# One idle step between the rounding and the transposes of the attention's output layer, for the first two batch elements

## The chip, the cores and the metric

The kernel runs on one core of one Trainium2 chip. The metric is the device time of one execution, in microseconds (us). The profile is one execution recorded by the hardware profiler. Engines: PE is TensorE (matmuls and transposes; PEld its weight loads), DVE is VectorE, ACT is ScalarE, POOL is GpSimd, SP issues DMAs. L231 is line 231 of the kernel before.

## The reference, cut to what matters

Four batch elements of 512 tokens by 512 channels pass through two layers, each with a mixing part and a feed-forward part, all residual:

```python
x = x + tanh(g_xattn[0]) * wkv(w, u, layernorm(x), ctx)                 # a recurrence over the tokens
x = x + tanh(g_ffn[0])   * bitlinear_ffn(layernorm(x), w1, w2, w3)      # 1-bit weights, int8 activations in groups of 64
x = x + tanh(g_xattn[1]) * cross_attention(layernorm(x), ctx)           # 16 heads of 32
x = x + tanh(g_ffn[1])   * ternary_linear(rmsnorm(layernorm(x)), W)     # ternary weights, int8 rows
```

The change concerns the end of the cross attention. Its output layer rounds each row of `o` to int8 levels before the product:

```python
def _qdq(x):
    s = jnp.maximum(jnp.max(jnp.abs(x), axis=-1, keepdims=True) / 127.0, 1e-08)
    return jnp.clip(jnp.round(x / s), -127.0, 127.0) * s
...
out = _qdq(o) @ _qdq(wp).T + bp
```

## The kernel before

Tokens lie on the 128 partitions, so one element is four row tiles t0 to t3 of 128 x 512. The four elements run as a pipeline: while the attention of element b is worked on, the feed-forward layer of element b+1 and the WKV recurrence of element b+2 run beside it. Every layer is a Python generator, and each `yield` ends a step. `line(generator, parts)` (L1190 to L1230) gives a generator a list of parts `(start, end, steps)`: step k of a part has the place `start + (end - start) * k / steps`. `run` always advances the line with the least place. One unit of place is one element, divided into `SLOTS` = 17 slots. The places set the order in which steps are written; `in_turn` and `next_turn` (L147 to L159) pin TensorE's instructions to that order, while the framework's scheduler may still order the other engines' instructions among themselves, by their dependences.

**The feed-forward layer** of the next element runs 16 units of one slot each: 8 up matmuls (`ff_hp`) for either branch, gating on ACT and DVE (`ff_z`, L745 to L750), transposes (`tp_ps`) with splitting into two fp32r parts (`hr`, ACT L696 and DVE L697), and 8 down matmuls (`ff_acc`). Its quantiser is `qg_s`, `qg_i`, `qg_b` (L671 to L685), the last step (`ff_z`/`ff_xn` back to float) on POOL. `xp` is the same kind of pair for the next row tile's input.

**The attention** works head by head: `s_ps` scores on TensorE, maximum `at_nm` on DVE (L948), exponential `at_P` on ACT (L950), transposes `pt_ps` with a copy `at_PT` on ACT (L970), values `o_ps` on TensorE with a copy on ACT (L990), a transpose back (`ot_ps`), division by the sums into `at_o` on DVE (L998, L1000). These 72 steps go over 18 slots. After them comes `project_out(t)` (L1017 to L1040), the output layer of one row tile, in three steps:

1. absolute maximum of the row (DVE L222), scale and reciprocal (DVE L226, L227), rounding in place (ACT L231, `at_o`);
2. four transposes into one PSUM bank (`qr_ps`) and their eviction to bf16 (ACT L238, `at_oqT`);
3. four bf16 matmuls (`p_ps`), scaling into `at_y` (DVE L1036), addition to the residual `xb` (POOL L1037 for elements 0 and 1).

`in_steps(chains, 1)` (L240 to L253) staggers the four row tiles by one step, the later tile first within a step. Three steps each, staggered by one, make 6 steps, which the part `(end, end + 2.4 / SLOTS, 6)` spreads over 2.4 slots. So in one step of the whole, t2 is rounded, t1 transposed, and t0 multiplied. Element 2 has an ending of its own with other places (`together`, `end`), element 3 runs with nothing beside it and has the same part of 6 steps.

**The ternary layer** of elements 0 and 1 (L1128 to L1180) follows: statistics of `xb` (DVE L191 to L206), power and normalisation on POOL (L180 to L219, L1147: `tf_xn`), absolute maximum (DVE L222, `tf_s`), rounding, transposes, product. Its line starts 11 slots (element 0) or 3 slots (element 1) after `end`.

**Buffers.** PSUM has eight banks: three with the tag "m", used in rotation by `qr_ps`, `p_ps`, `pt_ps`, `ot_ps`, `tp_ps`, `wy_ps`, `q_ps` and `o_ps`; three with "hp" (`s_ps` and `ff_hp`); two with "acc". An instruction that takes a bank waits for the instruction that last read it. `at_oqT` has two buffers; `at_y` shares the rotating row buffers `at_row` (`ROWS` of them) with `at_xn`, `at_q`, `at_half` and `tf_xn`; the small scale tiles `at_s` have four.

Of the kernel before, what the change touches and what calls it, by code (L numbers as in the profile page):

```python
# [30 lines left out]
def kernel(  # L31
# [37 lines left out]
    NB, T, D = x.shape  # L69
# [61 lines left out]
    def bank(name, dtype=F32):  # L131

        return psum_tile(name, "m", dtype)
# [27 lines left out]
    def matmul(*args, **kwargs):  # L161
        return in_turn(nc.tensor.matmul(*args, **kwargs))  # L162
# [58 lines left out]
    def absmax(dst, src):  # L221
        nc.vector.tensor_reduce(dst, src, AX.X, ALU.max, apply_absolute_value=True)  # L222

    def int8_scale(s, r, amax):

        nc.vector.tensor_scalar(s, amax, 1.0 / 127.0, 1e-8, ALU.mult, ALU.max)  # L226
        nc.vector.reciprocal(r, s)  # L227

    def rounded(src, r):

        nc.scalar.activation(src, src, AF.Identity, bias=magic[:, 0:1], scale=r)  # L231

    def transposed_rows(dst, src):

        pt = bank("qr_ps")
        for c in range(NC):
            transpose(pt[:, c * P : (c + 1) * P], src[:, c * P : (c + 1) * P], ident)
        nc.scalar.activation(dst, blocks(pt), AF.Identity, bias=magic[:, 1:2])  # L238
# [601 lines left out]
    def attention_layer(b, xb, pool, tiles=range(NT)):  # L840
# [15 lines left out]
        def row(name, dtype=F32):  # L856
            return pool.tile([P, D], dtype, name=name, tag="at_row", bufs=ROWS)
# [159 lines left out]
        def project_out(t):  # L1017
            s = sm.tile([P, 2], F32, name="at_s", tag="at_s")
            o = o_all[:, t, :]
            absmax(s[:, 0:1], o)  # L1020
            int8_scale(s[:, 0:1], s[:, 1:2], s[:, 0:1])
            rounded(o, s[:, 1:2])
            yield True
            oqT = pool.tile([P, NC, P], BF16, name="at_oqT", tag="at_oqT")
            transposed_rows(oqT, o)
            yield True
            pp = bank("p_ps")
            for c in range(NC):
                matmul(
                    pp, lhsT=oqT[:, c, :], rhs=wpT[:, c, :], start=(c == 0), stop=(c == NC - 1)  # L1030
                )
            if b > NB - 3:
                y = wk.tile([P, D], F32, name="at_y", tag="wk_v")
            else:
                y = row("at_y")
            nc.vector.scalar_tensor_tensor(y, pp, s[:, 0:1], swp_b, ALU.mult, ALU.mult)  # L1036
            (nc.vector if b > NB - 3 else nc.gpsimd).tensor_tensor(  # L1037
                xb[:, t, :], xb[:, t, :], y, ALU.add
            )
            yield True  # L1040
# [9 lines left out]
        def end(ts):  # L1050

            yield from together([project_out(t) for t in ts])
            means, scale = statistics(b, xb, ts)
            yield from together([ternary(b, xb, pool, t, means, scale) for t in ts])
# [51 lines left out]
        if alone:  # L1106
            yield from ending
        else:
            yield from in_steps([project_out(t) for t in tiles], 1)
# [66 lines left out]
    def ternary_layer(b, xb, pool):  # L1176
        if b == NB - 2:
            r, scale = statistics(b, xb, range(NT))
            yield
        else:  # L1180
            r, scale = layernorm(xb, rms=True, pinned=False), None
        yield from in_steps([ternary(b, xb, pool, t, r, scale) for t in range(NT)], 1)
# [9 lines left out]
    def late(make):  # L1192
        yield from make()
# [26 lines left out]
    SLOTS = NT * NF + 1  # L1220

    def line(gen, *parts, aside=False):
        lines.append({"gen": gen, "parts": parts, "step": 0, "aside": aside})
# [124 lines left out]
    for b in range(NB):  # L1348
        if b:
            early = (0.99, 1.0, 4) if b == 1 else (b - 0.19, b - 0.1, 3), (b - 0.08, b, 1)  # L1350
            line(
                late(lambda b=b: ffn_layer(xs[b])),
                *((early[0],) if b == 1 else early),
                (b, b + 16 / SLOTS, 64),
                (b + 16 / SLOTS, b + 17.75 / SLOTS, 7),
            )
        start = b + 1 + 4.95 / SLOTS
        end = start + 18 / SLOTS
        line(
            late(lambda b=b: attention_layer(b, xs[b], at)),  # L1360
            (b + 1.0 if b == 0 else b + 0.7, b + 1.03 if b == 0 else b + 0.9, 5),
            (b + 1 + 1.7 / SLOTS, b + 1 + 3.7 / SLOTS, 5),
            (b + 1 + 3.75 / SLOTS, b + 1 + 4.35 / SLOTS, 2),
            (start, end, 72),
            (end, end + 2.4 / SLOTS, 6)
            if b != NB - 2
            else (end - 0.15 / SLOTS, end + 4.65 / SLOTS, 6),
            (end + 2.4 / SLOTS, end + 3.4 / SLOTS, 4),
        )
        if b < NB - 1:  # L1370
            late_by = 8 / SLOTS if b == 0 else 0.0
            line(
                late(lambda b=b: ternary_layer(b, xs[b], at)),
                (end + 3 / SLOTS + late_by, end + 8 / SLOTS + late_by, 8)
                if b < NB - 2
                else (end + 4.85 / SLOTS, end + 11.85 / SLOTS, 7),
                aside=b < NB - 2,
            )
# [46 lines left out]
```

## Time and profile before

| what | value |
|---|---|
| median of 3 runs | 1088.22 us (1086.59, 1090.55, 1088.22) |
| the profiled execution, its own time | 1090.16 us |
| its span in the profile | 1088.2 us |
| its mean granted TensorE clock | 0.959 |
| PE busy | 942.7 us (87%) |
| PEld busy | 678.8 us (62%) |
| DVE busy | 828.3 us (76%) |
| ACT busy | 730.4 us (67%) |
| POOL busy | 322.1 us (30%) |
| chain that ended last | PE 46%, DVE 24%, ACT 14%, POOL 6%, DMA 5%, issue 5% |

The profiled execution is 1.94 us above the median and has 1.96 us around its span. "Busy" counts the time in which an engine works on an instruction; matmuls are pipelined, so their ends are modelled. In a timeline a row gives start, duration of the whole group, engine, line, operation, output <- input, the shapes and a count, and in brackets the idle time of the engine just before and the instruction that ended it. "PEclk" or granted clock is the share of full speed that TensorE's throttle allowed. The end of element 0's attention lies at 584 to 622 us of the span, that of element 1 at 796 to 820 us.

### The profile page before, as it was taken

The page shows a single profiled execution, that of the slowest core. Times are in us where ns is not written, and L with a number is a line of the kernel's source. Part 1 is how long each engine was busy: PE and PEld are TensorE (multiplying, and loading weights), DVE is VectorE, ACT ScalarE, POOL GpSimd, SP SyncE. Part 2 cuts the span into 40 slices and gives each one's busy share as a digit, 9 for nine tenths or more (in the row PEclk, how much of TensorE's full clock was granted, in tenths as well). Part 3 has the DMA queues.
Part 4 walks back from the last instruction along what each step waited for, and adds up shares of the span by engine and source line. Part 5 has one row for each costly group of instructions (what it writes and reads, how often), then busy time and mean ns, then how long its engine had stood idle before and what let it go on. Part 6 is the DMA issues. An engine that isn't in the chain of part 4 may idle for free.

```text
span 1088.2 us, 17928 instructions
## 1 busy us (share of the span) xinstructions
PE 942.7 (87%) x6351; PEld 678.8 (62%) x6380; DVE 828.3 (76%) x1600; ACT 730.4 (67%) x1490; POOL 322.1 (30%) x328
## 2 busy tenths in 40 slices
PE   3869997998978889889997898999999999878975
PEld 2335565565657666677775576777777777655652
DVE  5985548757876799897769799978687766579977
ACT  6656756566545776768777577777675767877863
POOL 3831104412433154621215536314022410100000
PEclk8889999998999999999999799999999999989998
DMA  8178945364454673745566446564683663244311
GB/s 290 39 254 323 327 167 205 136 221 166 155 138 164 229 252 103 257 117 158 211 204 211 146 150 200 155 235 146 221 242 117 207 215 93 73 132 118 115 41 39
DMA packets 85672, 189.67 MB, mean 174 GB/s; under 512 B 12240, under 2 KB 36816, under 8 KB 74576
## 3 DMA queue, kind: packets, MB, share of 16 engines
q1 hardware_dynamic: 85584, 188.53, 52.7%
q8 instruction: 51, 0.84, 0.3%
q14 instruction: 37, 0.30, 0.1%
HBM read 148.65 MB, written 39.85 MB: 173 GB/s over the span
## 4 chain that ended last, share of the span: by engine, by line
PE 46%; DVE 24%; ACT 14%; POOL 6%; DMA 5%; issue 5%; SPq 0%; ACTq 0%; POOLq 0%; DVEq 0%
PE ff_hp L162 13%; PE pt_ps L165 7%; PE ff_acc L162 5%; PE o_ps L162 4%; PE v_ps L162 4%; PE s_ps L162 3%; ACT at_P L950 3%; DVE wk_q L640 3%; DVE at_nm L948 3%; ACT at_PT L970 2%; PE k_ps L162 2%; DVE ff_z L750 1%; DVE qg_i L680 1%; DVE wk_p L634 1%; PE tp_ps L165 1%
## 5 line engine op out<-in xcount | busy, mean ns | idle before, releaser
L162 PE MATMUL ff_hp<-wT,xp 128*128 128x512 f32 x1024 | 273.9, 410 | 7.7 <-DVE ff_z L746 4.6
L162 PEld LDWEIGHTS ff_hp<-wT,xp 128*128 128x128 f32 x1024 | 194.1, 194 | 54.9 <-DVE ff_z L746 6.1
L950 ACT ACTIVATE at_P<-s_ps,at_nm 128x512 f32<-128x512 f32 x256 | 175.2, 691 | 45.3 <-DVE at_nm L948 43.6
L948 DVE TENSOR_REDUCE at_nm<-s_ps 128x1 f32<-128x512 f32 x256 | 166.5, 678 | 37.6 <-PE s_ps L162 37.3
L970 ACT COPY at_PT<-pt_ps 128x512 f32<-128x512 f32 x224 | 131.4, 591 | 73.3 <-PE pt_ps L165 72.6
L685 POOL TENSOR_TENSOR ff_z<-qg_b,qg_s 128x512 f32<-128x512 bf16 x64 | 72.7, 1135 | 314.6 <-ACT qg_b L684 291.0
L165 PE MATMUL pt_ps<-ident,at_P 128*128 128x128 f32 x1024 | 156.2, 282 | 9.0 <-ACT at_PT L970 4.9
L165 PEld LDWEIGHTS pt_ps<-ident,at_P 128*128 128x128 f32 x1024 | 119.1, 143 | 47.4 <-ACT at_PT L970 12.5
L162 PE MATMUL ff_acc<-wT,hr 128*128 128x512 f32 x512 | 137.1, 408 | 7.3 <-ACT hr L696 3.8
L162 PE MATMUL s_ps<-at_kR,at_qR 128*128 128x512 f32 x256 | 103.8, 467 | 27.4 <-ACT at_P L950 20.2
L162 PEld LDWEIGHTS ff_acc<-wT,hr 128*128 128x128 f32 x512 | 92.0, 189 | 28.7 <-DVE hr L697 5.6
L162 PE MATMUL o_ps<-at_PT,at_V 128*32 128x128 f32 x2048 | 75.6, 281 | 5.0 <-ACT at_PT L970 3.2
L162 PEld LDWEIGHTS o_ps<-at_PT,at_V 128*32 128x32 f32 x2048 | 55.0, 111 | 28.6 <-issue 11.4
L745 ACT ACTIVATE ff_z<-ff_hp,coef 128x512 f32<-128x512 f32 x64 | 44.1, 689 | 41.6 <-PE ff_hp L162 39.3
L746 DVE SCALAR_TENSOR_TENSOR ff_z<-ff_z,ff_hp 128x512 f32<-128x512 f32 x64 | 43.4, 678 | 37.2 <-ACT ff_z L745 36.8
L750 DVE SCALAR_TENSOR_TENSOR ff_z<-ff_hp,coef,ff_z 128x512 f32<-128x512 f32 x64 | 47.7, 746 | 29.2 <-PE ff_hp L162 28.8
L162 PEld LDWEIGHTS s_ps<-at_kR,at_qR 128*128 128x128 f32 x256 | 43.7, 195 | 41.6 <-ACT at_P L950 28.6
L684 ACT CAST qg_b<-qg_i 128x512 bf16<-128x512 int8 x80 | 49.3, 617 | 26.6 <-DVE qg_i L680 19.0
L162 PE MATMUL v_ps<-wkvT,cT 128*128 128x512 f32 x128 | 60.4, 618 | 5.6 <-DVE wT L303 2.3
L162 PE MATMUL k_ps<-cT,wkvT 128*128 128x512 f32 x128 | 60.5, 624 | 2.4 <-ACT wk_k L584 1.0
L640 DVE RECIPROCAL wk_q<-wk_q 128x256 f32<-128x256 f32 x32 | 54.5, 1722 | 2.9 <-POOL wk_q L635 1.5
L950 ACT ACTIVATION_READ_ACCUMULATOR at_P<-s_ps,at_nm 128x1 f32 x256 | 52.0, 203 | 0.0
(180 smaller groups left out, 1656.1 us busy)
## 6 DMA issues: line engine op xcount, KB each, us to landing
wT<-wD SPq DMA_DIRECT2D x72, 1024.0 KB, 5.6
wn<-in_L_ffn_w_dram SPq DMA_DIRECT2D x18, 1024.0 KB, 6.5
at_kR<-kD SPq DMA_DIRECT2D x128, 128.0 KB, 4.9
at_qR<-qD SPq DMA_DIRECT2D x256, 64.0 KB, 2.4
wD<-wT SPq DMA_DIRECT2D x12, 1024.0 KB, 4.5
kD<-k_half SPq DMA_DIRECT2D x16, 512.0 KB, 2.8
qD<-at_half SPq DMA_DIRECT2D x32, 256.0 KB, 2.1
cn<-in_ctx_dram SPq DMA_DIRECT2D x8, 512.0 KB, 6.2
```

What stands on the lines that cost most here:

```text
L162: return in_turn(nc.tensor.matmul(*args, **kwargs))
L165: return in_turn(nc.tensor.transpose(*args))
L634: nc.vector.tensor_tensor_scan(p[:, 1:], A2, E2, 0.0, ALU.mult, ALU.add)
L640: nc.vector.reciprocal(half, half)
L684: nc.scalar.copy(qb, qi)
L685: nc.gpsimd.tensor_tensor(grouped(src), grouped(qb), s.unsqueeze(2).to_broadcast([P, NG, GS]), ALU.mult)
L745: nc.scalar.activation(z, hp, AF.Tanh, scale=coef[:, 0:1])
L746: nc.vector.scalar_tensor_tensor(z, z, 1.0, hp, ALU.add, ALU.mult)
L750: nc.vector.scalar_tensor_tensor(z, hp, coef[:, 1:2], z, ALU.mult, ALU.mult)
L948: nc.vector.tensor_reduce(nm, sp, AX.X, ALU.max, negate=True)
L950: nc.scalar.activation(lanes[k, i, t], sp, AF.Exp, bias=nm, accum_out=sums[k][:, t, i : i + 1],)
L970: made[k] = nc.scalar.copy(dst, blocks(pt))
```

## The change

`project_out` gets one more `yield` after the rounding, for elements 0 and 1 only (`b < NB - 2`, with `NB` = 4). The step between the two yields holds no instruction. With four steps each, staggered by one, the four row tiles now make 7 steps, and the part is lengthened from 2.4 to 2.8 slots, so that a step still takes 0.4 of a slot. In one step of the whole, t3 is rounded, t2 does nothing, t1 is transposed and t0 is multiplied. Elements 2 and 3 keep their parts of 6 steps. The four leftover steps of the last part and the ternary layer's places are as before.

```diff
@@ project_out
             int8_scale(s[:, 0:1], s[:, 1:2], s[:, 0:1])
             rounded(o, s[:, 1:2])
             yield True
+            if b < NB - 2:
+                yield True
             oqT = pool.tile([P, NC, P], BF16, name="at_oqT", tag="at_oqT")
             transposed_rows(oqT, o)
             yield True
@@ the attention's line
             (start, end, 72),
-            (end, end + 2.4 / SLOTS, 6)
-            if b != NB - 2
+            (end, end + 2.8 / SLOTS, 7)
+            if b < NB - 2
+            else (end, end + 2.4 / SLOTS, 6)
+            if b == NB - 1
             else (end - 0.15 / SLOTS, end + 4.65 / SLOTS, 6),
             (end + 2.4 / SLOTS, end + 3.4 / SLOTS, 4),
```

## The prediction

> **What bounds the kernel now.** I read the table of engines first: TensorE is busy for 87% of the span, VectorE for 76%. The chain of waits over the whole span gives PE 46%, DVE 24%, ACT 14%: the bound changes hands. So the two places that the change touches were read by themselves: the end of element 0's attention (584 to 626 us) and of element 1's (796 to 835 us).
>
> TensorE's timeline at the first place (start, duration, tile, count; in brackets the idle time before it and what ended it):
>
> ```profile
> 594.90 0.60 PE L165 MATMUL wy_ps<-ident,wk_e 128*128 128x128 f32 x4
> 599.34 1.11 PE L165 MATMUL qr_ps<-ident,at_o 128*128 128x128 f32 x4 [3.84 <-ACT at_o L231]
> 600.25 1.91 PE L162 MATMUL p_ps<-wpT,at_oqT 128*128 128x512 bf16 x4
> 602.09 1.94 PE L162 MATMUL o_ps<-at_PT,at_V 128*32 128x128 f32 x32
> 603.96 0.95 PE L165 MATMUL pt_ps<-ident,at_P 128*128 128x128 f32 x4
> ...
> 612.02 0.63 PE L165 MATMUL tp_ps<-ident,ff_z 128*128 128x128 f32 x4 [0.66 <-ACT at_PT L970]
> 615.42 1.11 PE L165 MATMUL tp_ps<-ident,ff_xn 128*128 128x128 f32 x4 [2.78 <-DVE at_y L1036]
> 616.69 1.11 PE L165 MATMUL pt_ps<-ident,at_P 128*128 128x128 f32 x4 [0.15 <-DVE at_o L1000]
> 617.45 1.20 PE L162 MATMUL s_ps<-at_kR,at_qR 128*128 128x512 f32 x2
> 618.46 1.93 PE L162 MATMUL p_ps<-wpT,at_oqT 128*128 128x512 bf16 x4
> 619.83 3.06 PE L162 MATMUL ff_hp<-wT,xp 128*128 128x512 f32 x8
> ```
>
> The reader is to see two idle stretches. The first is the one the change is aimed at: the four transposes of a row tile stand in TensorE's queue right behind its rounding, and the rounding (L231) comes late, because the chain of waits there is on VectorE from 589 to 597.9 (0.41 us of it issue), then ScalarE's. After each stretch the same instructions last longer. The windows show why (columns: PE, PEld, DVE, ACT, POOL busy us with counts, granted clock, DMA share, GB/s):
>
> ```profile
> 595.00:600.00 5.00, 1.16 (x8) 0.92 (x7) 5.00 (x12) 4.57 (x9) 2.31 (x2) 0.78 0.74 255
> 600.00:605.00 5.00, 5.00 (x45) 3.02 (x44) 3.11 (x8) 3.32 (x7) 1.97 (x1) 0.54 0.86 168
> ...
> 615.00:620.00 5.00, 4.43 (x15) 2.68 (x15) 5.00 (x9) 2.22 (x4) 4.92 (x5) 0.50 0.42 149
> ```
>
> The clock is 0.54 and 0.50 where its neighbours (605 to 615) have 1.00 and 0.98. At the second place no transposes wait for a rounding; TensorE's waits before 822 us are 0.30, 0.47 and 0.39. Just behind it stands a loss of another kind:
>
> ```profile
> 828.15 0.50 PE L162 MATMUL s_ps<-at_kR,at_qR 128*128 128x512 f32 x1 [0.96 <-ACT at_P L950]
> 829.29 0.66 PE L165 MATMUL pt_ps<-ident,at_P 128*128 128x128 f32 x4 [0.64 <-ACT at_PT L970]
> 830.13 3.47 PE L162 MATMUL ff_hp<-wT,xp 128*128 128x512 f32 x8
> ```
>
> VectorE's timeline names its cause: at 825.34 it had waited 3.00 us for the ternary layer's tf_xn from GpSimd (L222 <- L1147), with the maxima of the scores queued behind.
>
> **The change, part by part.** No instruction or DMA is added or removed; counts are equal on every engine. The idle step and the seven steps at the same pace (2.4/6 = 2.8/7 = 0.4 of a slot) leave each rounding where it is and put transposes and products 0.4 of a slot later. In the changed program's order TensorE does, at the first place: wy, transposes t1, product t0, o_ps, pt, ff_acc, pt, s_ps, ff_hp, transposes t2, product t1, pt, ot, both tp, s_ps, pt, transposes t3, product t2, ff_hp, o_ps, pt, ff_acc, product t3. Elements 2 and 3 keep their code.
>
> *First place, what goes.* The idle time 3.84 + 0.66 + 2.78 + 0.15 = 7.43 us. Low clock: each slow row against the same form at full clock around 805 us (transposes 0.60, products 1.03, o_ps 1.08, s_ps 0.71, ff_hp 2.01). First run: 0.51 + 0.88 + 0.86 + 0.35 = 2.60. Second: 0.51 + 0.51 + 0.49 + 0.90 + 1.05 = 3.46. Together 13.5 us, the most that could go.
>
> *What comes.* Up to 595.2 VectorE's order is as before. From wy's start (594.90), by start-to-start spacings (transposes 0.44, product 0.9, o_ps 1.0) and with the wait for at_oqT, TensorE is through o_ps at about 598.1. The next pt takes the bank that xb<-wy_ps (L653) frees. L653 started at 599.64; now five 0.6 us VectorE instructions and a 1.2 us one (L680) stand ahead of it from 595.3, so it ends near 599.9: wait 1.8. The two scores after that start near 602.7 instead of 606.96. Transposes t2 and product t1 find their rounding done. Next, pt before transposes t3 needs the bank that hr (L697) frees, and t3 itself xp's; VectorE gets there behind at_y 0.65, L680 1.2, two WKV steps (L629 1.3, L632 0.6) and hr 0.6, that is 4.4 us after product t1's end near 606.5: pt at 610.9, with TensorE idle since 608.7, so 2.2, then 0.5 for xp, and 0.3 in small. New idle 4.8. A low clock after the second of these I take as likely, after the first as not: 3.0, the mean of 2.60 and 3.46. New loss 7.8, so TensorE gains 5.7 (8.7 without a drop, 2.6 with both).
>
> *What of it lasts.* Further on VectorE sets the pace:
>
> ```profile
> 640.00:645.00 5.00, 4.95 (x54) 3.72 (x53) 5.00 (x10) 4.54 (x10) 1.41 (x2) 1.00 0.23 67
> 645.00:650.00 5.00, 4.39 (x26) 3.49 (x23) 5.00 (x7) 3.11 (x8) 4.29 (x4) 1.00 0.54 138
> 650.00:655.00 5.00, 3.35 (x20) 2.37 (x18) 5.00 (x6) 2.57 (x7) 4.55 (x4) 1.00 0.99 406
> ```
>
> VectorE is full for 15 us, and the chain is on it from 639.5 to 653.5. A lead lasts there only as far as VectorE got idle time back before. It idles 1.89 + 2.58 + 0.50 + 0 + 1.12 = 6.1 us between 600 and 625 (windows); in my replay it still waits 0.5 for s_ps, 0.75 for ff_hp and some 1.3 besides, 2.5 in all. **I take −3.5 us.** Ends: −6.1, all of that idle time gone; above, three new waits as long as the 3.84 (11.5) and both low runs (6.1) against 13.5, which is +4.1.
>
> *Second place.* Transposes t3 and product t2 now stand ahead of a pt and two scores, behind hr and xp. Replayed from the rows: tp waits for at_y t1 0.6 (before 0.47), a pt 0.3 (before 0.30), t3 waits from 814.7 to 816.6 for hr behind L680, which took 1.49 there, and a statistics step: 1.9; product t2 0.25. That is 3.05 against 1.16: +1.9. A clock drop after it, at the size of the 3.47 row against 2.01: +1.46. In return at_y t3 comes seven us later, and in the new order VectorE's tf_s stands behind L948 and L746 instead of ahead of them; so the stall of 3.00 no longer holds the scores, and 0.96 + 0.64 + 1.46 = 3.06 goes. **Sum +0.3**; without the drop −1.2, with one of 3.46, +2.3.
>
> *The rest.* VectorE's and GpSimd's instructions change places by one or two in a dozen spots (WKV steps, ln_r against ff_z), and three key or weight loads pass an output store on SP's queue. No wait for those loads appears at the two places. I take 0, from −2 to +2: a lone wait such as 0.96 or 0.66, three times either way.
>
> Sum: −3.5 + 0.3 + 0 = −3.2, on the profiled execution 1090.16 − 3.2 = 1087.0. It stands 1.94 above the median of 1088.22; the same edit on the median gives **1085.0 us**.
>
> **Two rules of the Trainium skill.** The clock rows: waits of 0.96 and 0.64 with matmuls between them were followed by 0.67 of the clock (830 to 835), the wait of 3.84 by 0.54. "TensorE: Matmul & The Clock Gate", Part 1: The HAM clock gate, puts the drop after about 3.4 us of idleness, in windows that run freely. By it my new waits, 2.2 at most, would be free: the second place would stand at −1.2 and the sum at −4.7. The rows decide: shorter gaps were followed by a slow clock here.
> Against the change speaks "Perfetto Trace Analysis", Identifying the Most-Contended Engine: TensorE is to be judged by weight loads, not matmul busy time. Here weight loads take 62% and VectorE 76%; an order of TensorE that removes no VectorE work would by that rule bring nothing, sum 0. The row at 595 to 600 shows VectorE full, yet it idles 6.1 us in the next 25, and that is what I count.
>
> **Rivals.**
> *All of it lasts.* TensorE's 5.7 at the first place stays, because VectorE's order there defers WKV steps, and the second place has no drop (−1.2): 1088.2 − 6.9 = 1081.3. For it: TensorE runs unbroken from 619.83 to 645. Against: three full VectorE windows.
> *The wait only moves.* At the first place pt and transposes t3 wait for L653 and hr as long as they did for at_o and at_y, with both low-clock runs: TensorE gains 2.6, VectorE's later stretch returns 2, the second place gives +0.3: 1087.9. For it: 595 to 600 is VectorE's stretch whatever TensorE does.
> *Slower: the second place decides.* It had nothing to cure. Transposes t3 stand there in front of the scores; behind them TensorE waits 1.9 longer and cools (3.46), and tf_s, seven us later, holds VectorE as long as before at its new place, so the 3.06 stays. With 1 us from the first place: +1.9 + 3.46 − 1 = +4.4, 1092.6. It decides from the point where TensorE's new idle time between 812 and 820 passes the 3.06 behind it and the stall on tf_xn remains.
>
> **How the numbers follow.** Forecast (−3.2; own range 1081.5 to 1087.5) 0.50; all of it lasts 0.18; the wait moves 0.15; slower 0.17. A measurement of this kernel tells about 0.3% (3.3 us) from no change. Of the forecast 0.30 lies beyond that, with the 0.18: faster 0.48; 0.20 and 0.15 within: same 0.35; slower 0.17. The range 1080 to 1091 leaves out about 0.08 below and 0.12 above.
>
> **What would show it.** Right: no qr_ps<-ident,at_o row with a wait for ACT L231; 600 to 605 near full clock; a wait of 1 to 2.5 us at pt or qr_ps for hr or xp near 610; ff_hp of 619.83 some 3 to 5 us earlier, and 655 us's scores about 3.5 earlier; at the second place about 1.9 before t3, and no 3.00 wait on tf_xn. Wrong: a lead at 622 us that is gone by 655, a clock near 0.5 at both old places, or a second place that loses over 3 us.

## The result, and the profile after

| | before | after |
|---|---|---|
| median, 19 runs each | 1088.08 us (1084.28 to 1090.55) | 1091.77 us (1089.73 to 1094.5) |
| ratio of the times | | 1.0035, 95% interval 1.0026 to 1.0045 |
| profiled execution | 1090.16 us, span 1088.2 | 1090.03 us, span 1088.1 |
| mean granted clock in it | 0.959 | 0.968 |

The change costs 3.7 us; 3.2 us of gain were predicted. The two profiled executions are equally long only because that of before lies 2.1 us above its median and that of after 1.7 below. So the traces are compared stretch by stretch, and the total is read from the medians. A lower granted clock is not the cause: its mean over the 19 executions of after is 0.963, and over the 20 of before that were timed beside e1 to e4 it is 0.9625.

The page of after, its table of engines and the chain that ended last:

```profile
PE 936.3 (86%) x6349; PEld 673.1 (62%) x6380; DVE 830.0 (76%) x1600; ACT 728.0 (67%) x1490; POOL 318.4 (29%) x328
...
PE 43%; DVE 24%; ACT 15%; DMA 6%; issue 5%; POOL 5%; SPq 1%; ACTq 0%; DVEq 0%; POOLq 0%
```

TensorE has 6.4 us less busy time than before (936.3 against 942.7): fewer matmuls ran at a low clock. Nothing of it shows in the time, and part of it is chance: this execution had the highest granted clock of after's 19. The first place, in TensorE's timeline of after (start, duration, tile, count, and in brackets the idle time before and what ended it):

```profile
595.25 0.60 PE L165 MATMUL qr_ps<-ident,at_o 128*128 128x128 f32 x4
...
599.11 0.66 PE L165 MATMUL pt_ps<-ident,at_P 128*128 128x128 f32 x4 [1.09 <-DVE xb L653]
...
611.03 0.66 PE L165 MATMUL pt_ps<-ident,at_P 128*128 128x128 f32 x4 [2.42 <-DVE hr L697]
611.63 1.11 PE L165 MATMUL qr_ps<-ident,at_o 128*128 128x128 f32 x4
612.54 1.91 PE L162 MATMUL p_ps<-wpT,at_oqT 128*128 128x512 bf16 x4
613.89 2.71 PE L162 MATMUL ff_hp<-wT,xp 128*128 128x512 f32 x8
```

This is the predicted picture. The transposes of t1 no longer wait for their rounding (3.84 before). The two new waits are there, for the predicted instructions: 1.09 for L653 (1.8 predicted) and 2.42 for hr (2.2 predicted), and the second is followed by a low clock. The `ff_hp` that started at 619.83 starts 5.9 us earlier. The windows of after (columns as before: PE, PEld, DVE, ACT, POOL busy, granted clock, DMA share, GB/s):

```profile
595.00:600.00 5.00, 3.79 (x49) 2.62 (x49) 5.00 (x13) 4.99 (x11) 1.04 (x1) 1.00 0.74 258
600.00:605.00 5.00, 5.00 (x27) 4.00 (x27) 4.53 (x9) 5.00 (x11) 1.30 (x1) 1.00 0.91 189
...
610.00:615.00 5.00, 3.96 (x14) 2.71 (x15) 4.99 (x8) 2.73 (x7) 4.92 (x4) 0.66 0.32 136
...
650.00:655.00 5.00, 4.34 (x48) 3.29 (x49) 5.00 (x12) 3.27 (x8) 0.94 (x2) 1.00 0.07 15
```

The clock of 0.54 at 600 to 605 is 1.00, that of 0.50 at 615 to 620 is 1.00 too, and one low stretch is left, 0.66 at 610 to 615. The scores that started at 654.40 start at 650.66, 3.7 us earlier. Up to here the prediction holds.

To see where the lead goes, take one VectorE instruction that returns once per gating step, `ff_z<-ff_hp,coef,ff_z` (L750), and subtract before's start from after's, occurrence by occurrence: −6.20 at before's 610.6, −5.27 at 639.5, −3.74 at 654.1, −2.24 at 688.9, **+0.81 at 712.8**. Most of the lead is eaten between 654 and 713 us, in a stretch whose program text the change does not touch. The first bite, in VectorE's timeline of after:

```profile
670.14 1.75 DVE L640 RECIPROCAL wk_q<-wk_q 128x256 f32<-128x256 f32 x1 [1.02 <-POOL wk_q L635]
671.81 0.63 DVE L746 SCALAR_TENSOR_TENSOR ff_z<-ff_z,ff_hp 128x512 f32<-128x512 f32 x1
672.36 1.74 DVE L640 RECIPROCAL wk_q<-wk_q 128x256 f32<-128x256 f32 x1
```

and in TensorE's:

```profile
672.49 3.37 PE L162 MATMUL ff_hp<-wT,xp 128*128 128x512 f32 x8 [3.67 <-DVE ff_z L746]
```

The same spot of before, VectorE and then TensorE:

```profile
673.50 0.66 DVE L746 SCALAR_TENSOR_TENSOR ff_z<-ff_z,ff_hp 128x512 f32<-128x512 f32 x1
674.62 3.37 DVE L640 RECIPROCAL wk_q<-wk_q 128x256 f32<-128x256 f32 x2 [0.46 <-POOL wk_q L635]
```

```profile
674.22 2.12 PE L162 MATMUL ff_hp<-wT,xp 128*128 128x512 f32 x8 [0.92 <-DVE ff_z L746]
```

Before, the gating step L746 goes first, and VectorE waits for GpSimd's `wk_q` behind it. After, the first half of a WKV reciprocal (L640) stands ahead of L746. VectorE waits 1.02 us for GpSimd and then computes for 1.75 before it gates; TensorE waits 3.67 instead of 0.92, and its next eight matmuls take 3.37 instead of 2.12. By before's 679.0 the lead is down to 3.14, from 4.54 at 665.3: 1.4 us went in the stretch that holds this spot.

Two more bites of the same sort follow, TensorE's and then VectorE's row of after:

```profile
693.01 1.06 PE L162 MATMUL o_ps<-at_PT,at_V 128*32 128x128 f32 x26 [1.25 <-ACT at_PT L970]
```

```profile
703.36 0.69 DVE L222 TENSOR_REDUCE tf_s<-tf_xn 128x1 f32<-128x512 f32 x1 [2.22 <-POOL tf_xn L1149]
```

On ScalarE the copy `at_PT` (692.38) now stands behind the rounding of `at_xn` (L231) and behind `ff_xn` (L215), where before it stood ahead of both; the lead is 0.50 at 699.8. On VectorE `tf_s` waits for `tf_xn` ahead of `qg_s` and `hr`, where before it ran behind L746 at 709.54, without a wait.

At the second place, TensorE, VectorE and ScalarE of after:

```profile
814.20 0.63 PE L165 MATMUL tp_ps<-ident,ff_z 128*128 128x128 f32 x4 [0.47 <-DVE qg_s L676]
...
817.20 0.66 PE L165 MATMUL qr_ps<-ident,at_o 128*128 128x128 f32 x4 [1.94 <-DVE hr L697]
...
841.43 0.63 PE L165 MATMUL tp_ps<-ident,ff_z 128*128 128x128 f32 x4 [0.91 <-ACT at_PT L970]
```

```profile
814.40 1.55 DVE L680 TENSOR_TENSOR qg_i<-ff_z,qg_r 128x512 int8<-128x512 f32 x1
...
816.48 0.67 DVE L697 TENSOR_TENSOR hr<-tp_ps,hr 128x512 fp32r<-128x512 f32 x1
...
836.80 0.69 DVE L222 TENSOR_REDUCE tf_s<-tf_xn 128x1 f32<-128x512 f32 x1 [2.36 <-POOL tf_xn L1149]
```

```profile
838.15 0.81 ACT L231 ACTIVATE tf_xn<-tf_xn,magic,tf_s 128x512 f32<-128x512 f32 x1 [2.69 <-POOL ff_z L685]
838.88 0.56 ACT L970 COPY at_PT<-pt_ps 128x512 f32<-128x512 f32 x1
```

The 1.94 for hr is the predicted 1.9. The stall of VectorE on `tf_xn`, 3.00 at 825.34 before, is not gone: it is 2.36 at 836.80, with the rounding that needs it (ACT L231) in front of `at_PT`, for which TensorE then waits. (The bracket of L231 names GpSimd's `ff_z`, which ended at 837.78; `tf_s`, which L231 also reads, was ready at 838.06.)

### The profile page after: what moved, and what is told of

Read it like the earlier page. It is cut to its first block, busy times and chain, and to the rows that moved or that the text cites. A ratio compares the mean times of both kernels' runs of the same rounds, so it can differ in the third digit from the quotient of the medians.

```text
span 1088.1 us, 17925 instructions
## 1 busy us (share of the span) xinstructions
PE 936.3 (86%) x6349; PEld 673.1 (62%) x6380; DVE 830.0 (76%) x1600; ACT 728.0 (67%) x1490; POOL 318.4 (29%) x328
## 4 chain that ended last, share of the span: by engine, by line
PE 43%; DVE 24%; ACT 15%; DMA 6%; issue 5%; POOL 5%; SPq 1%; ACTq 0%; DVEq 0%; POOLq 0%
PE ff_hp L162 13%; PE pt_ps L165 6%; PE ff_acc L162 5%; PE o_ps L162 4%; ACT at_P L950 3%; PE s_ps L162 3%; DVE wk_q L640 3%; PE v_ps L162 3%; ACT at_PT L970 3%; DVE at_nm L948 3%; PE k_ps L162 2%; DMA at_qR<-qD 2%; DVE wk_p L634 2%; DVE qg_i L680 1%; PE tp_ps L165 1%
## 5 line engine op out<-in xcount | busy, mean ns | idle before, releaser
L746 DVE SCALAR_TENSOR_TENSOR ff_z<-ff_z,ff_hp 128x512 f32<-128x512 f32 x64 | 43.4, 679 | 34.9 <-ACT ff_z L745 34.6
L750 DVE SCALAR_TENSOR_TENSOR ff_z<-ff_hp,coef,ff_z 128x512 f32<-128x512 f32 x64 | 47.7, 745 | 28.3 <-PE ff_hp L162 28.2
L640 DVE RECIPROCAL wk_q<-wk_q 128x256 f32<-128x256 f32 x32 | 54.6, 1723 | 3.5 <-POOL wk_q L635 2.1
```

Source lines behind the costliest of these rows:

```text
L640: nc.vector.reciprocal(half, half)
L746: nc.vector.scalar_tensor_tensor(z, z, 1.0, hp, ALU.add, ALU.mult)
L750: nc.vector.scalar_tensor_tensor(z, hp, coef[:, 1:2], z, ALU.mult, ALU.mult)
```

## The experiments

Every kernel was timed in several rounds against before; medians from different rounds are best compared by their ratios. "Old" is six steps over 2.4 slots without the idle step. The last three columns are changes of the lead in the one profiled execution (us, minus is gained), by the VectorE row used above: first place 592 to 654, then 654 to 713, and second place 800 to 875. In e2_second_only the first column should be 0, since its program is before's up to there; it is −1.2, so this is what one execution can be off by.

| kernel | first place | second place | median us | ratio, 95% interval | 592–654 | 654–713 | 800–875 |
|---|---|---|---|---|---|---|---|
| after | idle, 2.8 | idle, 2.8 | 1091.77 | 1.0035 [1.0026, 1.0045] | −3.7 | +4.6 | +0.9 |
| e1_first_only | idle, 2.8 | old | 1090.25 | 1.0030 [1.0017, 1.0042] | −3.7 | +4.5 | +0.1 |
| e2_second_only | old | idle, 2.8 | 1090.89 | 1.0033 [1.0021, 1.0045] | −1.2 | 0.0 | +2.5 |
| e3_no_stretch | idle, 2.4 | idle, 2.4 | 1081.31 | 0.9943 [0.9929, 0.9956] | −5.2 | +1.3 | −3.6 |
| e4_stretch_only | 2.8 | 2.8 | 1080.57 | 0.9935 [0.9920, 0.9949] | −4.7 | 0.0 | −2.3 |
| f1_ffz_ahead | idle, 2.8, pinned | idle, 2.8 | 1087.04 | 1.0004 [0.9993, 1.0015] | −4.8 | +1.1 | +2.4 |
| f2_tfs_behind | idle, 2.8, tf_s held | idle, 2.8 | 1091.63 | 1.0041 [1.0028, 1.0054] | −2.6 | +4.5 | +2.4 |
| f4_second_alone | 2.8 | idle, 2.8 | 1088.55 | 1.0012 [1.0001, 1.0023] | −4.6 | 0.0 | +2.6 |
| f5_best_guess | 2.8 | idle, 2.4 | 1079.77 | 0.9940 [0.9927, 0.9953] | −4.6 | 0.0 | −3.6 |
| g1_second_250 | 2.8 | idle, 2.5 | 1079.77 | 0.9928 [0.9914, 0.9941] | −4.7 | 0.0 | −3.7 |
| g2_second_255 | 2.8 | idle, 2.55 | 1083.98 | 0.9967 [0.9956, 0.9978] | −4.6 | 0.0 | −0.6 |
| g3_first_changed_second_240 | idle, 2.8 | idle, 2.4 | 1087.97 | 0.9999 [0.9989, 1.0010] | −3.7 | +4.6 | −2.5 |
| g4_first_pinned_second_old | idle, 2.8, pinned | old | 1083.69 | 0.9963 [0.9950, 0.9977] | −5.0 | +1.2 | 0.0 |

**One place at a time.** The diffs of the first four kernels are against after.

```diff
# e1_first_only
-            if b < NB - 2:
+            if b == 0:
-            if b < NB - 2
+            if b == 0
-            if b == NB - 1
+            if b != NB - 2
```

> The idle step and the seven steps for element 0 alone; element 1 keeps its six. Theory G (given back): TensorE is 5 to 6 us ahead of the kernel before at 612 to 622 us, and all of it is lost again by 712 us in VectorE's and GpSimd's changed order (in the changed kernel's trace the lead falls from 6.2 at 610 to 0.5 behind at 712): the time ends at 0.5 to 2.5 us above before. Theory S (the second place carries the loss): first place alone gives 0 to 3 us less than before. Theory C (the granted clock): the time is within 1 us of before, and the runs' times differ by their mean clock alone.

```diff
# e2_second_only
-            if b < NB - 2:
+            if b == 1:
-            if b < NB - 2
+            if b == 1
-            if b == NB - 1
+            if b != NB - 2
```

> The idle step and the seven steps for element 1 alone; element 0 keeps its six. Up to 790 us it is the kernel before, so its trace there shows how much two executions of one order differ. Theory G: about 1 us above before (the changed trace goes from 0.5 behind at 796 us to 1.4 behind at 875). Theory S: 3 to 4.5 us above before, with TensorE's wait of 1.9 for hr ahead of the transposes of the last row tile. Theory C: within 1 us.

Either place alone costs as much as both together, 1.0030 and 1.0033 against 1.0035. So the loss is not the second place's alone, and not a first place that gained and was outweighed; nor do the two losses add.

**One half of the edit at a time.**

```diff
# e3_no_stretch
-            (end, end + 2.8 / SLOTS, 7)
+            (end, end + 2.4 / SLOTS, 7)
```

> The idle step for both elements, but the seven steps within the old 2.4 slots, so that a step takes 0.34 of a slot and the roundings come earlier. It tells whether the distance between rounding and transposes or the places behind them cost the time. Theory G: the local lead at 622 us stays near 5, the loss behind it depends on where VectorE's instructions fall: between 2 below and 4 above before. Theory S: the second place loses less, since the last transposes stand earlier: 0 to 2 above before.

```diff
# e4_stretch_only
-            if b < NB - 2:
-                yield True
...
-            (end, end + 2.8 / SLOTS, 7)
+            (end, end + 2.8 / SLOTS, 6)
```

> No idle step; six steps for both elements, spread over 2.8 slots. Transposes follow their rounding in the same step as before, but all comes up to 0.4 of a slot later. Theory G: the 3.84 wait for the rounding stays or grows, no lead at 622 us, 0 to 4 above before. Theory S: the last product moves later at the second place as in the changed kernel, with about the same loss: 2 to 4 above before.

Either half alone makes the kernel faster than before, by 6.2 us (e3) and 6.9 us (e4); the two halves together make it slower. They gain 4.7 (e4) and 5.2 us (e3) by 654, and keep all (e4) or most of it to 713. So a full VectorE does not by itself eat a lead. Nor does it take transposes that find their inputs ready: at the first place e4's transposes t3 wait 3.54, and the clock is 0.50 at 610 to 615.

```profile
610.89 1.12 PE L165 MATMUL qr_ps<-ident,at_o 128*128 128x128 f32 x4 [3.54 <-DVE hr L697]
```

**The order on VectorE pinned.** At the spot near 670 the kernels fall into two groups. In after, e1, f2 and g3 the first half of L640 stands ahead of L746, and TensorE's wait there is 3.59 to 3.69; in the others, as in before, L746 is first and the wait is 0.72 to 0.94.

The traces also give the whole order. VectorE starts 118 instructions between 654 and 713 us of before. Counting the places of this order that hold another instruction than in before: none in e2, e4, f4, f5, g1 and g2, where the lead loses nothing in this stretch; 26 in f1 and g4 (+1.1 and +1.2); 71 in e3 (+1.3); 74 in f2 (+4.5); 91 in after, e1 and g3 (+4.5 to +4.6). The count alone sets no price: e3 and f2 lie three places and 3.2 us apart, and of the two only f2 has L640 ahead of L746.

The pin, f1_ffz_ahead, queues the two reciprocals of each chunk of element 3's WKV behind the last gating step written before them. Nothing is left out of the computation. The diff is against after.

```diff
# f1_ffz_ahead
+    gated_by = []
...
-                nc.vector.reciprocal(half, half)
+                inverse = nc.vector.reciprocal(half, half)
+                if b == 3:
+                    behind(inverse, gated_by[-1])
...
-            nc.vector.scalar_tensor_tensor(z, z, 1.0, hp, ALU.add, ALU.mult)
+            gated_by.append(nc.vector.scalar_tensor_tensor(z, z, 1.0, hp, ALU.add, ALU.mult))
```

> The changed kernel with one order of VectorE pinned: both reciprocals of a WKV chunk of element 3 (L640) are queued behind the gate product ff_z (L746) that was written last before them. In the changed kernel the first reciprocal stood ahead of ff_z near 670 us, waited 1.02 for GpSimd, and TensorE waited 3.67 for ff_z. With the pin the scheduler also puts the copy at_PT ahead of at_xn on ScalarE near 690 us and the maxima tf_s behind ff_z near 710 us, as in the kernel before. Theory G (the lead of the first place is given back by these orders): the lead stays at 3 to 5 us at 713 us and the time falls by 3 to 5.5 us from the changed kernel's, to 1086 to 1089. Theory V (VectorE is full there, so the lead goes whatever the order): less than 1 us of change, about 1091. The second place is as in the changed kernel.

3.4 us come back by the ratios (1.0035 to 1.0004), 4.7 by the medians. VectorE and then TensorE of f1_ffz_ahead; its lines lie higher, L642 is L640 and L750 is L746:

```profile
670.44 0.66 DVE L750 SCALAR_TENSOR_TENSOR ff_z<-ff_z,ff_hp 128x512 f32<-128x512 f32 x1
671.56 3.37 DVE L642 RECIPROCAL wk_q<-wk_q 128x256 f32<-128x256 f32 x2 [0.46 <-POOL wk_q L637]
```

```profile
671.15 2.12 PE L164 MATMUL ff_hp<-wT,xp 128*128 128x512 f32 x8 [0.91 <-DVE ff_z L750]
```

The order, the wait and the clock are before's again, three microseconds earlier. The pin moves more than it names: with it `tf_s` also runs behind L746 again (707.61, no wait), and on ScalarE `at_PT` stands ahead of `at_xn` again. So it was asked what `tf_s` costs by itself:

```diff
# f2_tfs_behind
-            absmax(s[:, 0:1], xn)
+            largest = absmax(s[:, 0:1], xn)
+            if b == 0 and t < 2:
+                behind(largest, gated_by[47])
```

> The changed kernel with only the last of these orders pinned: the maxima tf_s of element 0's first two row tiles stand behind ff_z near 710 us, as before, instead of ahead of qg_s and hr, where VectorE waited 2.22 and 0.56 for tf_xn and TensorE 1.53 for hr. The order near 670 and 690 stays as changed. Theory G: 1 to 1.5 us less than the changed kernel, about 1090.5. Theory V: no change. A third reading, that this one order explains the whole loss, would give 5 us less.

It gained nothing: 1091.63. The stall at 703 is gone from its trace, and 654 to 713 still costs +4.5, lost earlier, with 3.59 at L746. The expectation failed; the wait on `tf_xn` only came last in a loss that was already made. What L640 and `at_PT` cost one without the other was not measured.

**The second place.** The diffs from here are against after, and f4's form stands for the others.

```diff
# f4_second_alone
-            if b < NB - 2:
+            if b in (1,):
...
-            (end, end + 2.8 / SLOTS, 7)
-            if b < NB - 2
+            (end, end + 2.8 / SLOTS, 6)
+            if b == 0
+            else (end, end + 2.8 / SLOTS, 7)
+            if b == 1
# f5_best_guess: the same, with  end + 2.4 / SLOTS, 7
# g1_second_250: the same, with  end + 2.5 / SLOTS, 7
# g2_second_255: the same, with  end + 2.55 / SLOTS, 7
```

> Element 0 with the stretch alone (six steps over 2.8 slots, no idle step), which kept a lead of 4.4 us; element 1 with the changed code. It prices the changed second place behind a good first one. Theory G: the second place loses what it lost alone, 0.9 to 2.5 us by the two traces, instead of the 2.3 that the stretch gained there: 1083.5 to 1085.5. If the loss at the second place were only due to the state in which element 0 leaves the queues, it would be the 1080.6 of the stretch in both.

> Element 0 with the stretch alone (it kept 4.4 us in its trace), element 1 with the idle step inside the old 2.4 slots (it gained 3.5 us there in its trace, because the last transposes stand ahead of the two tp and wait for nothing). If the two places add up: 7.9 us below before, 1079.5 or a little less. If what follows depends on the orders that the scheduler finds anew: anywhere from 1080 to 1086.

f4 came out worse than expected: seven steps over 2.8 slots instead of six, for element 1 alone, take 1088.55 against e4's 1080.57, and f5's 2.4 gives all of it back. The next two kernels differ by a twentieth of a slot. Transposes t3 come after five of the seven steps: at 1.79 slots behind the attention's end with 2.5, at 1.82 with 2.55. The feed-forward step with two `tp_ps` stands at 1.80.

> Element 0: no idle step, six steps over 2.8 places; element 1: idle step, seven steps over 2.5 places. At 2.5 the third tile's transposes (5/7 of 2.5 = 1.79 places after the attention's end) still stand ahead of the feed-forward step at 1.80 whose two tp_ps wait for at_y. Order theory (what costs at the second place is that the third tile's transposes and the second's product stand behind that feed-forward step): like the run with 2.4 there, 1080 to 1082, and no wait of 1.9 for hr. Pace theory (each later tenth of a place costs a little): between the runs with 2.4 (1079.8) and 2.8 (1088.6), near 1082 to 1083.

> As the run with 2.5, with 2.55 places for element 1: the third tile's transposes come at 1.82, now behind the feed-forward step at 1.80. Order theory: a jump of at least 3.4 us over the run with 2.5 (wait 1.9 for hr, low clock after it 1.5), up to 8 if all that the run with 2.8 lost hangs on this one swap: 1084 to 1089. Pace theory: within 1 us of the run with 2.5.

The jump that the order theory asked for is there: 1079.77 and 1083.98, 4.2 us for 0.05 slots (intervals [0.9914, 0.9941] and [0.9956, 0.9978]), and nothing between 2.4 and 2.5. A second loss of about the same size, 0.9967 to 1.0012, lies between 2.55 and 2.8 and was not narrowed down. TensorE of g1, g2 and f4:

```profile
809.51 0.60 PE L165 MATMUL qr_ps<-ident,at_o 128*128 128x128 f32 x4
810.23 1.02 PE L162 MATMUL p_ps<-wpT,at_oqT 128*128 128x512 bf16 x4
811.09 0.60 PE L165 MATMUL tp_ps<-ident,ff_z 128*128 128x128 f32 x4
811.53 0.60 PE L165 MATMUL tp_ps<-ident,ff_xn 128*128 128x128 f32 x4
```

```profile
808.67 0.66 PE L165 MATMUL tp_ps<-ident,ff_xn 128*128 128x128 f32 x4
809.94 0.66 PE L165 MATMUL qr_ps<-ident,at_o 128*128 128x128 f32 x4 [0.62 <-DVE hr L697]
```

```profile
809.37 0.60 PE L165 MATMUL tp_ps<-ident,ff_xn 128*128 128x128 f32 x4
811.91 0.66 PE L165 MATMUL qr_ps<-ident,at_o 128*128 128x128 f32 x4 [1.94 <-DVE hr L697]
812.63 1.48 PE L162 MATMUL p_ps<-wpT,at_oqT 128*128 128x512 bf16 x4
813.90 1.06 PE L165 MATMUL pt_ps<-ident,at_P 128*128 128x128 f32 x4
814.61 1.20 PE L162 MATMUL s_ps<-at_kR,at_qR 128*128 128x512 f32 x2
815.61 2.42 PE L162 MATMUL ff_hp<-wT,xp 128*128 128x512 f32 x8
```

In g1 the transposes (`qr_ps`) stand ahead of the two `tp_ps` and wait for nothing. In g2 they stand behind and wait 0.62, in f4 1.94. Behind f4's wait the next four groups take 0.45 + 0.46 + 0.49 + 0.42 = 1.8 us more than at full clock (1.03, 0.60, 0.71, 2.00), and its windows show the clock:

```profile
810.00:815.00 5.00, 3.03 (x13) 2.15 (x14) 3.62 (x7) 1.95 (x5) 1.18 (x3) 0.81 0.91 346
815.00:820.00 5.00, 5.00 (x49) 3.78 (x49) 2.76 (x5) 3.26 (x8) 1.25 (x1) 0.85 0.20 82
```

In g2 only 0.6 of the 4.2 us is that wait; g1 and g2 also differ in VectorE's order behind it, and in the waits at 856 to 859 (0.85 in g1; 1.11 + 0.41 + 0.73 in g2). In TensorE's order here the swap is all that sets both apart; how its price splits was not taken further. The swap need not cost: e4's six steps over 2.8 slots put transposes t3 at 1.87, behind the same two `tp_ps`, where they wait 0.61, and e4 gains 2.3 us at this place. Its row:

```profile
810.01 0.66 PE L165 MATMUL qr_ps<-ident,at_o 128*128 128x128 f32 x4 [0.61 <-DVE hr L697]
```

So the jump is shown, and what of the orders behind it costs the time is not.

**Do the two places add?** The diffs are against after; the second keeps f1's pin.

```diff
# g3_first_changed_second_240
-            if b < NB - 2
+            if b == 0
+            else (end, end + 2.4 / SLOTS, 7)
+            if b == 1
# g4_first_pinned_second_old: f1's pin, and
-            if b < NB - 2:
+            if b in [0]:
-            if b < NB - 2
+            if b == 0
+            else (end, end + 2.4 / SLOTS, 6)
+            if b == 1
```

> The changed code at element 0 (idle, seven steps over 2.8), and at element 1 the idle step with seven steps over 2.4. If the losses of the two places add: 1091.8 less the 5 to 8.8 us that 2.4 instead of 2.8 at the second place was worth, 1083 to 1087. If the loss at the first place is made anew by whatever second place follows (the element-0-alone run took 1090.3): 1089 to 1091.

> The changed code at element 0 with VectorE's two WKV reciprocals (L640) of element 3 queued behind the last gating step (L746); element 1 as before the change. If the WKV order is what ate the first place's lead: 1090.25 of the element-0-alone run less 4.7 = 1085.5, faster than before by 1.5 to 3. If the 4.7 of the pinned changed kernel came from the second place by way of the downstream order: 1089 to 1091.

g3's 1087.97 lies between the two expectations, just outside the first: 3.8 us below after, where the same edit of the second place took f4 down by 8.8 to f5, behind a first place that kept its lead. In its trace the first place repeats after's to a tenth, −3.7 and +4.6. g4 came out better than expected, 1083.69: the pin alone turns the first place from 3.3 us slower than before (e1, 0.0030 of 1087.5) into 4.0 us faster (0.0037). With the old second place the pin is worth about 7 us, with the changed one 3.4 (both by the ratios).

The lowest medians are those of f5_best_guess and g1_second_250: no idle step for element 0, an idle step and seven steps over 2.4 or 2.5 slots for element 1. At 0.9940 [0.9927, 0.9953] and 0.9928 [0.9914, 0.9941] they beat both kernels; between these two, e3 and e4 nothing can be told apart.

## Why the prediction was wrong

- **What bounds the kernel now, and what goes at the first place: right.** 7.43 us of idle time and both low-clock runs are gone; the new waits and the one low run came where they were placed.
- **"What of it lasts ... I take −3.5 us": right at 654 us (−3.7), by luck.** The reason does not carry. VectorE's three full windows do not eat a lead: f1, g4, e4, f4, f5, g1 and g2, whose order on VectorE is before's there, lose 0.2 us or nothing between 639 and 654. After loses 1.5 there, with its own order of WKV steps.
- **"The rest ... I take 0, from −2 to +2": the step that failed.** "VectorE's and GpSimd's instructions change places by one or two in a dozen spots", and one of them, L640 ahead of L746 at 670, comes with a loss of 4.5 us between 654 and 713 in all four kernels that have it; the pin, with the orders that follow it, takes 3.4 of these away (f1, +1.1). The bound was taken from lone waits of before, 0.66 and 0.96. What it missed is that a swap on VectorE can make TensorE wait for a whole reciprocal, 3.67 instead of 0.92, that a low clock follows (0.80 at 670 to 675), and that later orders differ too: 91 of VectorE's 118 places between 654 and 713 hold another instruction. The prediction had looked at the program's order on VectorE; it has L640, L746, L640 where that of before has L746, L640, L640.
- **"Second place ... Sum +0.3": its waits right, its gain wrong.** 1.94 came for 1.9, and low clock in four of the five traces with the changed second place. But "the stall of 3.00 no longer holds the scores, and 3.06 goes" failed: the stall moved with `tf_s` to 836.80 (2.36) and holds scores and ScalarE's copies there. Four traces put the place at +2.4 to +2.6; after's own, with no low clock there, at +0.9.
- **The rivals.** "Slower: the second place decides" had this place right, with the moved stall and the cooling, and its 1092.6 is the nearest of all to 1091.8. It had not that the first place gives all of its gain back. "All of it lasts" described the first place of e4 and f5, not of the change.
- **The signs to look for** were all read at or near the two places. Up to 655 us the rows asked for came as described, the `ff_hp` even 5.9 us earlier instead of 3 to 5; the time still went the other way.
- **The sum.** First place +0.9 (−3.7 + 4.6) and second place +2.5 make +3.4 beside 3.7 measured. That is no proof: the same sum for f4, −4.6 + 2.6 = −2.0, stands beside +1.3 (1.0012), and e1 alone costs 3.3 for +0.9. From 938 us to the end VectorE, ScalarE and GpSimd keep before's order in every kernel, and still the traces differ from before's by −3.1 (g1) to −0.1 us (g2); the timed executions of one kernel differ by 1 to 7 us. Single traces are no finer than that. Why the two places do not add stays open.

## What to carry to other kernels

When a scheduler may reorder the other engines, an edit of one engine's order is an edit of every queue downstream: compare the changed program's order on each engine over the whole pipeline, and price every swap that puts a long instruction, or one that waits for a third engine, ahead of one that TensorE waits for. Watch the lead by one recurring instruction over the whole span rather than the edited place, because a lead of 6 us can be gone 100 us later. In a hand-written order, look for thresholds: a step that passed a neighbour with late inputs (1.79 to 1.82 slots) came with 4.2 us, while 2.4 and 2.5 slots could not be told apart. But time the whole kernel: with other steps around it (e4) the same swap came with a gain.

## What the runs showed of the hardware

- The same 1.94 us wait with the same instructions behind it was followed by a clock of 1.00 in after's windows (810 to 820), 0.81 and 0.85 in f4's, and 0.69 in e2's at 815 to 820 (wait 1.93). The Trainium skill, "TensorE: Matmul & The Clock Gate", Part 1: The HAM clock gate, tells of windows that run freely, which agrees with some executions being hit and others not. It puts the fall of the clock after about 3.4 us of idleness; here a single wait of 1.93 or 1.94 us was enough.
- L680 (512 columns, fp32 to int8) takes 0.69 us on average where GpSimd is idle or overlaps it by no more than 0.3 us (58 of 80 in after, none over 0.77), and up to 1.55 beside a GpSimd instruction. At 809.11 in f4 it took 1.55 behind GpSimd's addition that ran from 808.84 to 810.11; in g1 it started first (811.96), took 0.68, and the addition took 1.68 instead of 1.28. The Trainium skill, "SBUF — State Buffer", SBUF: two separate sides, tells of a pair of ports that VectorE and GpSimd share and that the first comer locks for a whole instruction, for a VectorE instruction with two inputs in SBUF, like L680, against a GpSimd instruction that reads SBUF; both rows agree. This 0.86 is part of the 1.94 that TensorE waits for hr.
